# Choice of attention heads split over three steps, weight loads spread between block moves, and v evacuated by ScalarE and POOL, in a four-layer attention and MoE kernel

## The chip, the cores and the metric

The kernel runs on one core of one Trainium2 chip. The metric is device time in microseconds (us), lower is better. The core's engines are TensorE (PE, with its weight loads shown apart as PEld), VectorE (DVE), ScalarE (ACT), GpSimd (POOL) and SyncE (SP), which here only issues DMAs and loads registers.

## The reference, cut to what matters

The input is x of 2 batches x 1024 tokens x 256 features. Four layers, each with a layer norm ahead and a residual add behind, run one after the other: (a) cross attention of 16 heads to 77 context tokens, (b) a self attention that chooses 4 of 16 heads for each batch, (c) a GELU layer whose two weight matrices are the context, (d) a top-1 mixture of 8 experts. The change concerns (b):

```python
def _L0_ffn_ref(x, Wq, bq, Wk, bk, Wv, bv, Wr, br, Wo, bo):   # x: layer norm of the residual, (2, 1024, 256)
    dist = softmax(mean(x @ Wr + br, axis=1), axis=-1)          # one distribution over 16 heads for each batch
    _, idx = top_k(dist, 4)
    idx = sort(idx, axis=-1)
    Q, K, V = proj(Wq, bq), proj(Wk, bk), proj(Wv, bv)          # 16 heads of 64
    Qs, Ks, Vs = gather(Q), gather(K), gather(V)                # the 4 chosen heads of each batch
    score = softmax(einsum('bhqd,bhkd->bhqk', Qs, Ks) / 8, axis=-1)
    O = einsum('bhqk,bhkd->bhqd', score, Vs)
    return O.transpose(0, 2, 1, 3).reshape(b, s, 256) @ Wo + bo
```

A batch's heads can be chosen only when all its 1024 tokens have left layer (a); the kernel then loads the weights of the four chosen heads only.

## The kernel before

**Tiling.** Tokens are cut into 16 tiles of 128 (8 for each batch), which lie in SBUF as `xs`. Layer (a) is a pipeline of 20 calls `a_step(s)` (L507): each runs the scores of tile s, the transposes of tile s-1, the values of tile s-2, the output's transpose of tile s-3 and its projection `po_a` of tile s-4 (added into `xs` by VectorE, L505). Layer (b) is a pipeline of 36 calls `b_step(s)` (L821). Its unit i is one query tile of 128 with one pair of heads, 32 units in all: sixteen of the first batch, then sixteen of the second. Layers (c) and (d) are pieces spread over the b-steps; the expert blocks (L1199 to L1230) come after the last one. The program is one straight line of instructions on each engine.

**What b_step(s) does, in order.** PE: scores of unit s (`bsc`, L721, four matmuls of 512 columns into two PSUM buffers of tag `big`). VectorE: transposes in place, in 32x32 blocks, of the second head of unit s-1 (`be`, L748). In every second step: the move of two units' transposed weights from `be` to `beT` across partitions, 16 DMAs issued by SP (`b_moved`, L750 to L761), and reciprocals of the softmax sums, spread by POOL (`brb`, L781). Then the evacuations that stand in the list `due`, which the step before put there, on ACT. Then for each of the two heads VectorE's negated row maximum (`bnm`, L737) and ACT's exponential from PSUM into `be` (L739). Then PE's values of unit s-4 (`bov`, L769, 64 matmuls that read `beT` and `v`) and VectorE's normalization (`boT`, L797). Every second step PE turns the sums (`brt`) and multiplies a finished tile by the output weights (`po_b`). Last, VectorE transposes the first head of unit s. `be` and `beT` have two buffers each, so the move before last must have read `be` before exponentials can write it again; the PSUM tags `big`, `tr` and `acc` have two buffers each, and `bov`, `po_b` and `v` share `acc`.

**What sets the order.** It is written out by hand. `at(stage, s, pos, f, ...)` (L1281) puts a call in the plan, `take` (L1284) runs the calls of a position: position 0 comes after the `due` evacuations and ahead of the exponentials, 2 behind the values, 3 ahead of the step's last transposes. `piece(f, ...)` (L1321) runs the PE part of f at once and appends its evacuation to `due`, so that it runs at the next step's start. The Python order is the order of each engine's queue.

**The choice of heads.** `route_sums` (L542) and `route_mean` (L551) sum a batch's normalized rows; `route_logits` (L559) multiplies by the router and takes the exponential; `route_heads` (L572) does the rest on VectorE: `rp`, `lg`, `top`, `idx` (L574 to L580), the sort of four indices by rank (L582 to L599), then on SP, for each chosen head, a register load (L609) and one DMA of 64 KB for each of k, q and v (L614) and one for the bias of v (L625), 16 in all, and last on VectorE the chosen heads' biases by a one-hot sum (`hot`, `hb`, `hs_`, `bc`, L628 to L645). For the first batch this is planned in a-step 14, for the second in b-step 3. The weights' tiles `ws_k`, `ws_q`, `ws_v` and `bvs` have one buffer each.

**q, k and v.** `b_qk(b, k, m, n)` (L648) makes 512 tokens of q or k for head pair m in one PSUM bank by two matmuls, evacuated with bias by ACT. `b_v(b, t)` (L674) makes v of one tile for all four heads; with `later` ACT copies it out of PSUM (L692) and POOL adds the bias (L693), without it VectorE does both in one add (L688). The second batch's v goes the first way, the first batch's the second way. The first batch's scores begin with b-step 0, the second's with b-step 16; values follow four steps later.

Of the kernel before, what the change touches and what calls it, by code (L numbers as in the profile page):

```python
# [9 lines left out]
F32 = mybir.dt.float32  # L10
# [8 lines left out]
SP = (mybir.EngineType.SP,)  # L19

P = 128
# [18 lines left out]
def kernel(  # L40
# [30 lines left out]
    nc = tc.nc  # L71
# [3 lines left out]
    C = D // P  # L75
# [13 lines left out]
    NH = f_wr.shape[1]  # L89
    FD = f_wq.shape[1] // NH  # L90
    NA = f_wo.shape[0] // FD
# [24 lines left out]
    wsp = early.enter_context(tc.tile_pool(name="wsp", bufs=1))  # L116
# [94 lines left out]
    for c0, c1, off0 in ((0, NCH - 1, 0), (NCH - 1, NCH, off_c[-1])):  # L211
        hs = hsel[:, c0:c1, :]
# [359 lines left out]
    def route_heads(b):  # L572

        lg, sm = sel[b]  # L574
        rp = small.tile([P, 1], F32, name=f"rp_{b}", tag="rp")
        nc.vector.reciprocal(rp, sm)
        nc.vector.tensor_scalar(lg, lg, rp, None, ALU.mult)
        top = small.tile([P, 8], F32, name=f"top_{b}", tag="top")
        idx = small.tile([P, 8], U32, name=f"idx_{b}", tag="idx")
        nc.vector.max(top, lg)  # L580
        nc.vector.max_index(idx, top, lg)

        fi = small.tile([P, NA], F32, name=f"fi_{b}", tag="fi")
# [17 lines left out]
        w = {  # L601
            k: wsp.tile([P, C, NA, FD], F32, name=f"ws_{k}{b}", tag=f"ws_{k}") for k in "qkv"
        }
        bv = wsp.tile([P, NA, FD], F32, name=f"bvs_{b}", tag="bvs")
        hs = {}

        def load(s, *what):
            if s not in hs:
                hs[s] = nc.values_load(seli[0:1, s : s + 1], engines=SP, min_val=0, max_val=NH - 1)  # L609
            for k in what:  # L610
                v = {"k": f_wk, "q": f_wq, "v": f_wv}[k].rearrange(
                    "(c p) (h d) -> p c h d", p=P, h=NH
                )
                nc.sync.dma_start(w[k][:, :, s : s + 1, :], v[:, :, bass.ds(hs[s], 1), :])  # L614

        load(0, "k", "q")
        load(1, "k", "q")
        load(2, "k")
        load(3, "k", "q")
        load(2, "q")  # L620
        for s in range(NA):
            load(s, "v")
        v = f_bv.rearrange("(h d) -> h d", h=NH)
        for s in range(NA):
            nc.sync.dma_start(bv[:, s, :], v[bass.ds(hs[s], 1), :].to_broadcast([P, FD]))  # L625
# [12 lines left out]
        nc.vector.tensor_reduce(  # L638
            hs_.rearrange("p k m h -> p (k m h)"), hb.rearrange("p k s n -> p (k s) n"),
            AX.X, ALU.add,  # L640
        )
        bc = wsp.tile([P, 2, NP], F32, name=f"bc_{b}", tag="bc", bufs=2)
        for h in range(2):
            r = slice(h * FD, h * FD + FD)
            nc.vector.tensor_copy(bc[r], hs_[r, :, :, h])  # L645
        sel[b] = w, {"k": bc[:, 0, :], "q": bc[:, 1, :]}, bv

    def b_qk(b, k, m, n, pool=accp, ptag="acc", later=False):  # L648

# [631 lines left out]
    def at(stage, s, pos, f, *args):  # L1281
        plan.setdefault((stage, s, pos), []).append((f, args))
# [70 lines left out]
    stages = [("a", s) for s in range(T + 4)] + [("b", s) for s in range(1, NI)]  # L1353
    for b in range(B):
        for i in range(4):
            s = b * NT + 2 * i + 5
            t0 = b * NT + 2 * i
            at(*stages[s], 3, do_rows, "b", t0, fbo_b)
            at(*stages[s + 1], 3, do_turn, "b", t0)
            at(*stages[s + 2], 1 if stages[s + 2][0] == "a" else 3, route_sums, b, i)  # L1360
        s = b * NT + 13
        at(*stages[s], 1 if b == 0 else 3, route_mean, b)
    at("a", 13, 3, route_logits, 0)
    at("a", 14, 1, route_heads, 0)
    at("b", 3, 2, route_logits, 1)
    at("b", 3, 3, route_heads, 1)
    for s, args in (
        (15, (0, "k", 0, 0)), (16, (0, "k", 0, 512)), (16, (0, "q", 0, 0)), (17, (0, "k", 1, 0)),
        (17, (0, "k", 1, 512)), (18, (0, "q", 1, 0)),
# [1 line left out]
        at("a", s, 3, b_qk, *args)  # L1371
    tr = (trp, "tr")
    acc = (accp, "acc")
    at("b", 2, 3, b_qk, 0, "q", 0, 512)
    at("b", 3, 3, b_qk, 0, "q", 1, 512)
    for t in range(NT):
        at(*(("a", 18, 3), ("a", 18, 3), ("b", 0, 3), ("b", 0, 3),
             ("b", 1, 2), ("b", 1, 3), ("b", 2, 2), ("b", 2, 3))[t], b_v, 0, t, *(acc if t > 3 else tr))
    for s, k, m, n in (
        (5, "k", 0, 0), (6, "k", 0, 512), (6, "q", 0, 0), (7, "k", 1, 0), (8, "k", 1, 512),  # L1380
        (9, "q", 1, 0), (18, "q", 0, 512), (20, "q", 1, 512),
    ):
        at("b", s, 3, piece, b_qk, 1, k, m, n, *tr)
    for t in range(NT):
        at("b", (10, 12, 13, 14, 15, 16, 17, 18)[t], 3, piece, b_v, 1, t, *acc)

    gelus = {}

# [9 lines left out]
    for g in range(3):  # L1398
        s, t0 = 4 * g, TG * g
# [13 lines left out]
    for t0 in (6, 8):  # L1413
        s = 2 * t0
# [12 lines left out]
    t0 = T1 - 2  # L1427
# [16 lines left out]
    t0 = T1  # L1444
# [197 lines left out]
```

## Time and profile before

| | us |
|---|---|
| median of 3 runs (lowest, highest) | 607.15 (604.54, 609.48) |
| the profiled execution: its time, its span | 606.1, 604.4 |
| PE busy (share of the span) | 536.2 (89%) |
| PEld busy | 408.3 (68%) |
| VectorE busy | 378.8 (63%) |
| ScalarE busy | 206.7 (34%) |
| POOL busy | 176.2 (29%) |
| mean granted PE clock | 0.935 of full speed |
| exponentials (L739), 64, each | 1.114 |
| row maxima (L737), 64, each | 1.212 |
| block transposes (L748), 64, each | 1.221 |
| values `bov` (L769), 1024 matmuls, each | 0.291 |
| scores `bsc` (L721), 256 matmuls, each | 0.661 |

The profile is of one execution; the span runs from its first to its last instruction, and all times "at" some point are counted from the span's start. Busy times are sums of the instructions' durations. "A <- B" in the waits reads: idle time of A's group that ended when B finished; the numbers behind it are the total, the count and the longest, in us. "x16" behind a row is the number of instructions in it. A granted clock of 0.50 means that PE ran at half speed in that stretch.

### The profile page before, as it was taken

Reading aid. Unit: us, or ns where it says so; the run is one execution under the profiler, and the core shown is the slowest. Engines: PE = TensorE matmul, PEld = TensorE weight load, DVE = VectorE, ACT = ScalarE, POOL = GpSimd, SP = SyncE. Lnnn points to the kernel's source line nnn. Section 1 sums busy time; section 2 is a strip of 40 time slices with the busy share of each in tenths; the row PEclk is TensorE's granted clock in tenths of the full one; section 3 lists DMA queues with packets and bytes.
Section 4 is the critical chain, followed back from the end, with each engine's and each line's share of the span. In section 5 each row is a group of like instructions: output and inputs, shape, how many; then the busy total and the mean of one; then the engine's idle time right before and its main releaser. Section 6 shows DMA issues by size and latency. Waiting matters only on the chain. (4 is left out here: it accounts for less than half of the span.)

```text
span 604.4 us, 10406 instructions
## 1 busy us (share of the span) xinstructions
PE 536.2 (89%) x3706; PEld 408.3 (68%) x3706; DVE 378.8 (63%) x894; ACT 206.7 (34%) x440; POOL 176.2 (29%) x225
## 2 busy tenths in 40 slices
PE   5999999989896599999998995794896899999994
PEld 4577878876444355666755563584786799999994
DVE  6767667862788367888888898765356233333341
ACT  3555555543343244555554443210210011111110
POOL 6646233433200001344623412003110232333221
PEclk9999999999987799999999996857797899999998
DMA  8000000020062956787686884569954599999940
GB/s 252 22 2 1 1 1 2 1 56 7 2 139 59 207 127 154 166 183 187 142 199 154 199 208 104 136 145 334 375 197 165 193 338 325 355 376 352 351 145 15
DMA packets 61707, 96.34 MB, mean 159 GB/s; under 512 B 15352, under 2 KB 46547, under 8 KB 61653
## 3 DMA queue, kind: packets, MB, share of 16 engines
q1 hardware_dynamic: 58384, 87.61, 51.9%
q0 software_dynamic: 2560, 7.34, 3.3%
q8 instruction: 31, 0.51, 0.4%
q10 hardware_dynamic: 709, 0.68, 0.3%
q14 instruction: 23, 0.19, 0.1%
HBM read 55.76 MB, written 6.82 MB: 104 GB/s over the span
## 5 line engine op out<-in xcount | busy, mean ns | idle before, releaser
L739 ACT ACTIVATE be<-bsc,bnm 128x1024 f32<-128x1024 f32 x64 | 71.3, 1114 | 107.3 <-DVE bnm L737 88.8
L737 DVE TENSOR_REDUCE bnm<-bsc 128x1 f32<-128x1024 f32 x64 | 74.9, 1212 | 23.6 <-PE bsc L721 23.6
L769 PEld LDWEIGHTS bov<-beT,v 128*64 128x64 f32 x1024 | 61.0, 147 | 36.0 <-issue 22.9
L721 PE MATMUL bsc<-kT,qT 64*128 64x512 f32 x256 | 76.0, 661 | 6.3 <-ACT be L739 6.3
L769 PE MATMUL bov<-beT,v 128*64 128x128 f32 x1024 | 68.8, 291 | 11.5 <-DMA beT<-be 7.9
L1218 PE MATMUL epo<-w2s,ehT 128*128 128x256 f32 x320 | 77.9, 387 | 0.0
L1199 PE MATMUL ph<-ybT,w1s 128*128 128x128 f32 x640 | 76.9, 278 | 1.0 <-DVE ybT L1184 1.0
L1199 PEld LDWEIGHTS ph<-ybT,w1s 128*128 128x128 f32 x640 | 76.0, 194 | 2.4 <-DVE ybT L1184 1.4
L748 DVE STREAM_TRANSPOSE be<-be 128x1024 f32<-128x1024 f32 x64 | 75.8, 1221 | 1.6 <-DMA beT<-be 1.1
L1206 ACT ACTIVATE ehT<-ph,b1s 128x128 f32<-128x128 f32 x80 | 22.9, 369 | 120.3 <-PE ph L1199 120.3
L1218 PEld LDWEIGHTS epo<-w2s,ehT 128*128 128x128 f32 x320 | 59.2, 195 | 6.8
L721 PEld LDWEIGHTS bsc<-kT,qT 64*128 64x128 f32 x256 | 27.5, 198 | 37.9 <-issue 18.0
L1208 DVE TENSOR_SCALAR ehT<-ph,b1s 128x128 f32<-128x128 f32 x80 | 22.5, 343 | 48.8 <-ACT ehT L1206 48.6
L1230 POOL DMA_INDIRECT out_dram<-ob,etok x20 | 20.4, 1018 | 93.9 <-DMA out_dram<-ob,etok 37.3
L478 PE MATMUL av<-vblk,eT 128*128 128x51 f32 x320 | 37.4, 272 | 0.8 <-DVE hn L486 0.8
L478 PEld LDWEIGHTS av<-vblk,eT 128*128 128x128 f32 x320 | 37.1, 192 | 1.6 <-DVE hn L486 1.1
L454 DVE TENSOR_REDUCE mx<-sc 128x8 f32<-128x616 f32 x32 | 25.3, 792 | 16.6 <-PE sc L440 16.6
L781 POOL COPY brb<-brc 128x256 f32<-128x256 f32 x16 | 6.4, 400 | 97.1 <-DVE brc L779 97.1
L470 ACT COPY eT<-pt 128x512 f32<-128x512 f32 (+1 forms) x48 | 23.0, 515 | 25.9 <-PE pt L469 25.3
L456 DVE TENSOR_TENSOR e<-sc,mx 128x616 f32<-128x616 f32 x32 | 25.6, 799 | 1.7
L291 POOL TENSOR_TENSOR rs_b<-rs_b,minus_half 128x2 f32<-128x2 f32 x8 | 5.7, 713 | 71.7 <-DVE rs_b L290 53.7
L460 ACT ACTIVATE e<-e 128x616 f32<-128x616 f32 x32 | 23.0, 723 | 9.4 <-DVE e L456 9.3
(260 smaller groups left out, 818.2 us busy)
## 6 DMA issues: line engine op xcount, KB each, us to landing
beT<-be SPq DMA_DIRECT2D x256, 128.0 KB
w1s<-in_L_ffn_w_dram SPq DMA_DIRECT2D x20, 1024.0 KB
w2s<-in_L_ffn_w_dram SPq DMA_DIRECT2D x20, 1024.0 KB
b2s<-in_L_ffn_b_dram SPq DMA_DIRECT2D x20, 128.0 KB
xs<-in_x_dram SPq DMA_DIRECT2D x4, 512.0 KB
ztok<-y_d SPq DMA_DIRECT2D x8, 256.0 KB
ztok<-xs SPq DMA_DIRECT2D x8, 256.0 KB
ws_k<-in_L_ffn_Wk_dram SPq DMA_DIRECT2D x8, 64.0 KB
```

The source lines that it names most:

```text
L454: nc.vector.tensor_reduce(mx, scv, AX.X, ALU.max)
L456: nc.vector.tensor_tensor(em.rearrange("p (g h) k -> p g h k", g=2), scv, mx.unsqueeze(3).to_broadcast([P, 2, HG, KC]), ALU.subtract,)
L460: nc.scalar.activation(em, em, AF.Exp)
L470: copy(eTs[t][:, c0 : c0 + n, :], pt[:, :n, :])
L478: nc.tensor.matmul(av[:, h0 : h0 + HW, :].rearrange("p h d -> p (h d)"), lhsT=eT[:, c, :], rhs=vblk[:, t // NT, c].rearrange("p h d -> p ( ...
L721: nc.tensor.matmul(sc[h][:, n : n + 512], lhsT=qks[b, "q", m][r, q0 : q0 + P], rhs=qks[b, "k", m][r, n : n + 512], start=True, stop=True,)
L737: nc.vector.tensor_reduce(nm, sc[h], AX.X, ALU.max, negate=True)
L739: nc.scalar.activation(bes[gm][:, :, q, h, :], sc[h].rearrange("p (g x) -> p g x", g=QD), AF.Exp, bias=nm, accum_out=sms[g][:, q, s : s + 1],)
L748: nc.vector.transpose(e, e)
L769: nc.tensor.matmul(ov[h * FD : (h + 1) * FD, :].rearrange("p (g x) -> p g x", g=QD), lhsT=vs[g * TG // NT][:, k, 2 * m + h, :], rhs=eT[:, ...
L1199: nc.tensor.matmul(ph[:, f, :], lhsT=ws[n][0][:, c, f * P : (f + 1) * P], rhs=ybT[:, c, :], start=(c == 0), stop=(c == C - 1),)
L1218: nc.tensor.matmul(po, lhsT=hT[:, f, :], rhs=w2s[:, f, :], start=(f == 0), stop=(f == FC - 1))
```

## The change

There are four edits.

- `route_heads` becomes a generator in parts. For the first batch all its parts are still taken in a-step 14. For the second batch the logits move from position 2 of b-step 3 to position 0; the choice of the indices is taken at (4, 0), the sort at (4, 2), the biases `hot` to `bc` at (5, 2), then the loads of the four k heads with their register loads at (6, 0), of q at (8, 0), of v at (10, 0) and of the bias of v at (12, 0). A generator's step runs up to the next `yield`, so the part up to `idx` is the first `next`, and so on. Position 0 of an even step comes behind the move that the same step issues.
- For the first batch k and q are loaded head by head, then v; the biases `hot` to `bc` are computed ahead of the loads for both batches.
- The first batch's v tiles all become pieces: two in a-step 18, two each in b-steps 0, 1 and 2, evacuated by ACT and POOL. Its last two q groups move from b-steps 2 and 3 to pieces in 4 and 5. The transposes of second-batch rows (`do_turn "b"`) that fall in b-steps become pieces too.
- The second batch's k and q groups move from steps 5, 6, 6, 7, 8, 9, 18, 20 to 8, 9, 10, 12, 13, 14, 20, 22, its v tiles from 10, 12, 13, 14, 15, 16, 17, 18 to 13, 13, 14, 15, 16, 17, 17, 19.

```diff
@@ -579,6 +579,7 @@
         idx = small.tile([P, 8], U32, name=f"idx_{b}", tag="idx")
         nc.vector.max(top, lg)
         nc.vector.max_index(idx, top, lg)
+        yield
 
         fi = small.tile([P, NA], F32, name=f"fi_{b}", tag="fi")
         nc.vector.tensor_copy(fi, idx[:, :NA])
@@ -598,11 +599,34 @@
         seli = small.tile([P, NA], I32, name=f"seli_{b}", tag="seli")
         nc.vector.tensor_copy(seli, se)
 
+        yield
+
+        hot = wsp.tile([P, NA, NH], F32, name=f"hot_{b}", tag="hot", bufs=1)
+        nc.vector.tensor_tensor(
+            hot, iota16.unsqueeze(1).to_broadcast([P, NA, NH]),
+            se.unsqueeze(2).to_broadcast([P, NA, NH]), ALU.is_equal,
+        )
+        hb = wsp.tile([P, 2, NA, NH], F32, name=f"hb_{b}", tag="hb", bufs=1)
+        nc.vector.tensor_tensor(
+            hb, hot.unsqueeze(1).to_broadcast([P, 2, NA, NH]),
+            hbT.unsqueeze(2).to_broadcast([P, 2, NA, NH]), ALU.mult,
+        )
+        hs_ = wsp.tile([P, 2, NP, 2], F32, name=f"hs_{b}", tag="hs", bufs=1)
+        nc.vector.tensor_reduce(
+            hs_.rearrange("p k m h -> p (k m h)"), hb.rearrange("p k s n -> p (k s) n"),
+            AX.X, ALU.add,
+        )
+        bc = wsp.tile([P, 2, NP], F32, name=f"bc_{b}", tag="bc", bufs=2)
+        for h in range(2):
+            r = slice(h * FD, h * FD + FD)
+            nc.vector.tensor_copy(bc[r], hs_[r, :, :, h])
+        yield
         w = {
             k: wsp.tile([P, C, NA, FD], F32, name=f"ws_{k}{b}", tag=f"ws_{k}") for k in "qkv"
         }
         bv = wsp.tile([P, NA, FD], F32, name=f"bvs_{b}", tag="bvs")
         hs = {}
+        sel[b] = w, {"k": bc[:, 0, :], "q": bc[:, 1, :]}, bv
 
         def load(s, *what):
             if s not in hs:
@@ -613,37 +637,15 @@
                 )
                 nc.sync.dma_start(w[k][:, :, s : s + 1, :], v[:, :, bass.ds(hs[s], 1), :])
 
-        load(0, "k", "q")
-        load(1, "k", "q")
-        load(2, "k")
-        load(3, "k", "q")
-        load(2, "q")
-        for s in range(NA):
-            load(s, "v")
+
+        for ks in (("k", "q"), ("v",)) if b == 0 else ("k", "q", "v"):
+            for s in range(NA):
+                load(s, *ks)
+            if b:
+                yield
         v = f_bv.rearrange("(h d) -> h d", h=NH)
         for s in range(NA):
             nc.sync.dma_start(bv[:, s, :], v[bass.ds(hs[s], 1), :].to_broadcast([P, FD]))
-
-        hot = wsp.tile([P, NA, NH], F32, name=f"hot_{b}", tag="hot", bufs=1)
-        nc.vector.tensor_tensor(
-            hot, iota16.unsqueeze(1).to_broadcast([P, NA, NH]),
-            se.unsqueeze(2).to_broadcast([P, NA, NH]), ALU.is_equal,
-        )
-        hb = wsp.tile([P, 2, NA, NH], F32, name=f"hb_{b}", tag="hb", bufs=1)
-        nc.vector.tensor_tensor(
-            hb, hot.unsqueeze(1).to_broadcast([P, 2, NA, NH]),
-            hbT.unsqueeze(2).to_broadcast([P, 2, NA, NH]), ALU.mult,
-        )
-        hs_ = wsp.tile([P, 2, NP, 2], F32, name=f"hs_{b}", tag="hs", bufs=1)
-        nc.vector.tensor_reduce(
-            hs_.rearrange("p k m h -> p (k m h)"), hb.rearrange("p k s n -> p (k s) n"),
-            AX.X, ALU.add,
-        )
-        bc = wsp.tile([P, 2, NP], F32, name=f"bc_{b}", tag="bc", bufs=2)
-        for h in range(2):
-            r = slice(h * FD, h * FD + FD)
-            nc.vector.tensor_copy(bc[r], hs_[r, :, :, h])
-        sel[b] = w, {"k": bc[:, 0, :], "q": bc[:, 1, :]}, bv
 
     def b_qk(b, k, m, n, pool=accp, ptag="acc", later=False):
 
@@ -1356,14 +1358,26 @@
             s = b * NT + 2 * i + 5
             t0 = b * NT + 2 * i
             at(*stages[s], 3, do_rows, "b", t0, fbo_b)
-            at(*stages[s + 1], 3, do_turn, "b", t0)
+            if stages[s + 1][0] == "a":
+                at(*stages[s + 1], 3, do_turn, "b", t0)
+            else:
+                at(*stages[s + 1], 3, piece, do_turn, "b", t0)
             at(*stages[s + 2], 1 if stages[s + 2][0] == "a" else 3, route_sums, b, i)
         s = b * NT + 13
         at(*stages[s], 1 if b == 0 else 3, route_mean, b)
     at("a", 13, 3, route_logits, 0)
-    at("a", 14, 1, route_heads, 0)
-    at("b", 3, 2, route_logits, 1)
-    at("b", 3, 3, route_heads, 1)
+    heads = {}
+
+    def route_part(b):
+        if b not in heads:
+            heads[b] = route_heads(b)
+        next(heads[b], None)
+
+    for _ in range(4):
+        at("a", 14, 1, route_part, 0)
+    at("b", 3, 0, route_logits, 1)
+    for s, pos in ((4, 0), (4, 2), (5, 2), (6, 0), (8, 0), (10, 0), (12, 0)):
+        at("b", s, pos, route_part, 1)
     for s, args in (
         (15, (0, "k", 0, 0)), (16, (0, "k", 0, 512)), (16, (0, "q", 0, 0)), (17, (0, "k", 1, 0)),
         (17, (0, "k", 1, 512)), (18, (0, "q", 1, 0)),
@@ -1371,18 +1385,18 @@
         at("a", s, 3, b_qk, *args)
     tr = (trp, "tr")
     acc = (accp, "acc")
-    at("b", 2, 3, b_qk, 0, "q", 0, 512)
-    at("b", 3, 3, b_qk, 0, "q", 1, 512)
+    for s, m in ((4, 0), (5, 1)):
+        at("b", s, 3, piece, b_qk, 0, "q", m, 512, *tr)
     for t in range(NT):
-        at(*(("a", 18, 3), ("a", 18, 3), ("b", 0, 3), ("b", 0, 3),
-             ("b", 1, 2), ("b", 1, 3), ("b", 2, 2), ("b", 2, 3))[t], b_v, 0, t, *(acc if t > 3 else tr))
+        s = ("a", 18) if t < 2 else ("b", t // 2 - 1)
+        at(*s, 3, piece, b_v, 0, t, *(tr if t < 2 else acc))
     for s, k, m, n in (
-        (5, "k", 0, 0), (6, "k", 0, 512), (6, "q", 0, 0), (7, "k", 1, 0), (8, "k", 1, 512),
-        (9, "q", 1, 0), (18, "q", 0, 512), (20, "q", 1, 512),
+        (8, "k", 0, 0), (9, "k", 0, 512), (10, "q", 0, 0), (12, "k", 1, 0), (13, "k", 1, 512),
+        (14, "q", 1, 0), (20, "q", 0, 512), (22, "q", 1, 512),
     ):
         at("b", s, 3, piece, b_qk, 1, k, m, n, *tr)
     for t in range(NT):
-        at("b", (10, 12, 13, 14, 15, 16, 17, 18)[t], 3, piece, b_v, 1, t, *acc)
+        at("b", (13, 13, 14, 15, 16, 17, 17, 19)[t], 3, piece, b_v, 1, t, *acc)
 
     gelus = {}
```

More of the change, by code (lines that the diff above doesn't have):

```diff
@@ L599, in route_heads @@
         nc.vector.tensor_copy(seli, se)
[L601 to L612, printed above, removed]
-                )
-                nc.sync.dma_start(w[k][:, :, s : s + 1, :], v[:, :, bass.ds(hs[s], 1), :])
-        load(0, "k", "q")
-        load(1, "k", "q")
-        load(2, "k")
-        load(3, "k", "q")
-        load(2, "q")
-        for s in range(NA):
-            load(s, "v")
-        v = f_bv.rearrange("(h d) -> h d", h=NH)
-        for s in range(NA):
-            nc.sync.dma_start(bv[:, s, :], v[bass.ds(hs[s], 1), :].to_broadcast([P, FD]))
+        yield
         hot = wsp.tile([P, NA, NH], F32, name=f"hot_{b}", tag="hot", bufs=1)
@@ L645, in route_heads, with load @@
             nc.vector.tensor_copy(bc[r], hs_[r, :, :, h])
-        sel[b] = w, {"k": bc[:, 0, :], "q": bc[:, 1, :]}, bv
+        yield
+        w = {
+            k: wsp.tile([P, C, NA, FD], F32, name=f"ws_{k}{b}", tag=f"ws_{k}") for k in "qkv"
+        }
+        bv = wsp.tile([P, NA, FD], F32, name=f"bvs_{b}", tag="bvs")
+        hs = {}
+        sel[b] = w, {"k": bc[:, 0, :], "q": bc[:, 1, :]}, bv
+        def load(s, *what):
+            if s not in hs:
+                hs[s] = nc.values_load(seli[0:1, s : s + 1], engines=SP, min_val=0, max_val=NH - 1)
+            for k in what:
+                v = {"k": f_wk, "q": f_wq, "v": f_wv}[k].rearrange(
+                    "(c p) (h d) -> p c h d", p=P, h=NH
+                )
+                nc.sync.dma_start(w[k][:, :, s : s + 1, :], v[:, :, bass.ds(hs[s], 1), :])
+        for ks in (("k", "q"), ("v",)) if b == 0 else ("k", "q", "v"):
[3 more added lines that the diff above has]
+                yield
+        v = f_bv.rearrange("(h d) -> h d", h=NH)
+        for s in range(NA):
+            nc.sync.dma_start(bv[:, s, :], v[bass.ds(hs[s], 1), :].to_broadcast([P, FD]))
     def b_qk(b, k, m, n, pool=accp, ptag="acc", later=False):
```

## The prediction

> **What bounds the kernel now.** I read the share of each engine by slices first, then a sum by stretches, then the waits, then SP's and VectorE's rows around the one hole. I call step s the call `b_step(s)` and date it by its first `bnm` (L737): steps 0 to 12 start at 154.42, 161.91, 170.35, 176.89, 186.64, 192.94, 200.04, 216.81, 223.58, 230.17, 236.07, 242.43, 247.25 us, step 13 at 254.66, step 18 at 285.73, step 24 at 328.04. Step 6 lasts 16.8 us, where the others last 5 to 8.
>
> ```profile
> 152.40:216.80 64.40, 48.80 (x223) 25.06 (x224) 42.32 (x70) 20.79 (x38) 5.61 (x7) 0.84 0.50 112
> 216.80:297.60 80.80, 79.95 (x643) 52.27 (x643) 68.21 (x97) 43.17 (x87) 27.17 (x34) 1.00 0.74 164
> ```
>
> The columns are the length, then the busy time of PE, PEld, DVE, ACT and POOL, then PE's clock, DMA share and rate. After 216.8 PE is busy 79.95 of 80.80 us: there PE's work sets the time. Before it PE idles 15.6 us and runs partly at half clock. So what an edit saves before 216.8 counts only less the PE work that it pushes behind that point.
>
> ```profile
> DVE boT L797 <- PE bov L769: 11.1, 4, 8.9
> PE bov L769 <- DMA beT<-be: 7.9, 2, 7.5
> PE bsc L721 <- ACT be L739: 6.3, 3, 4.7
> ```
>
> The hole is PE waiting 7.5 us for a move (`beT<-be`), with VectorE waiting 8.9 us behind it. The 4.7 us are one step before: scores 5 wait for the exponentials of step 4. Why both, the timelines of SP and VectorE show (start, time from the first to the last of the group, instruction):
>
> ```profile
> 169.51 10.12 SPq L758 DMA_DIRECT2D beT<-be  x16
> 183.98 0.39 SPq L614 DMA_DIRECT2D ws_k<-in_L_ffn_Wk_dram  x1
> ...
> 193.58 1.91 SPq L625 DMA_DIRECT2D bvs<-in_L_ffn_bv_dram  x4
> 195.59 10.06 SPq L758 DMA_DIRECT2D beT<-be  x16
> ```
>
> The timeline of VectorE over the same stretch:
>
> ```profile
> 176.89 2.31 DVE L737 TENSOR_REDUCE bnm<-bsc 128x1 f32<-128x1024 f32 x2
> 179.13 0.15 DVE L565 TENSOR_TENSOR lg<-rps,br_b 128x16 f32<-128x16 f32 x1
> ...
> 184.29 2.37 DVE L748 STREAM_TRANSPOSE be<-be 128x1024 f32<-128x1024 f32 x2
> ```
>
> VectorE chooses the heads from 179.13 to 184.29 (5.16 us), and the transposes of step 3 wait behind it. Move 1 is ready at 186.6, but SP issues 16 weight and bias loads until 195.5, so it goes out at 195.59 and has landed by 207.5. A move costs SP 10.1 us (16 issues, one each 0.63 us).
>
> [...] the trace has clock 0.50 in 163.5 to 170.2, 187.4 to 194.1 and 204.5 to 211.1, each after PE idling. [...] v leaves PSUM by ScalarE and POOL adds the bias after; second batch's v does so here (374 ns L692, 732 ns L693).
>
> **The change, part by part.**
>
> First batch's v. Eight adds of 419 ns leave VectorE (about 0.34 us each in the queue, 2.7 us) for eight ACT copies of 374 ns and eight POOL adds of 732 ns, hidden on engines that are 34% and 29% busy. But the copies stand behind the step's exponentials on ACT. Copies 2 and 3 use the `acc` buffers, so `po_a` of the last attention tile now waits for copy 2: exponentials of step 0 end at 158.03, copy 158.4, `po_a` (1.03) 159.45, and VectorE's add (L505, at 159.08 before) 159.5. The two v adds saved in step 0 are eaten: step 1 at 162.35 (+0.45). In step 1 PE does both v tiles after `lps_b`, whose rows POOL delivers at 164.6; two tiles of 1.85 us at half clock, then scores 2: step 2 at 171.4 (+1.05). Were PE at full clock there, 169.3; I take 171.4 and keep 2 us for the range. Step 2 loses one 0.34 add twice but gets the two small logits operations and waits for them: 6.4 us, step 3 at 177.8.
>
> Choice of heads in three parts. Step 3 keeps 0.94 us of the 5.16 (reciprocal to index, 180.76 to 181.70), after its transposes. Exponentials of step 3 end at 181.45, transposes at 182.65: move 1 is ready at 182.65, 3.9 us sooner, and SP is empty (move 0 done about 177.4). Step 4 starts at 183.65. Step 4: bnm 2.27, boT 0.22, second part 1.4 (181.72 to 183.04 and its gap), transposes 2.3: 6.2. Step 5: 2.27, 0.22, third part 1.25, 2.3, reciprocal: 6.1. Steps 5 and 6 start at 189.85 and 195.95. The two q matmul groups that come to steps 4 and 5 (1.81 each) fit, PE having 3.8 of 6.2 us to do. Move 1 lands at 182.7 + 10.1 + 1.8 = 194.6 (1.8 from last issue to use, 205.65 to 207.5), before it is needed: the 7.5 and 4.7 us are gone. Step 6 has then only 4.9 us of VectorE work: step 7 at 200.85 against 216.81, 16.0 us sooner.
>
> Loads behind the moves. Each kind must go out before the next move. From before: a k head with its register load 1.16 us (186.77 to 187.93), four 4.65; q, v 0.555 each, four 2.2; bias 0.525, four 2.1. Move 2 is ready at 195.95 and issues to 206.15, landing 207.95. k goes to 210.8; move 3 is ready by 205.8 but goes 210.9 to 221.3, landing 223.1; q to 223.5, move 4 to 233.9, landing 235.7; v to 236.1 (one slow issue of 1.3 could add 1), move 5 to about 247, landing 248.7. Who waits: `bov` of steps 8, 10 and 12, and the exponentials of those steps, whose `be` buffer the move two before must have left. PE at step 8 is through its scores at 206.1 and waits 1.85 us; then po_b 0.87, k 1.81 (landing taken as in time; batch 0's were used 3.4 us after issue, a bound of 1.3 us late), scores 1.92: step 9 at 214.2. Step 10 at 220.1, `bov` waits for 223.1; step 11 at 229.0; step 12 at 234.1 (13.2 sooner), `bov` waits 1.4 for 235.7; step 13 at 243.0 (11.7 sooner). Move 5 meets no waiter.
>
> Work moved later. From step 13 on PE carries what before was done: k and q of head pair 1 (two groups of 1.81) and two v tiles of 0.96, so 5.5 us. Summing PE by rows (bsc 1.92 + bov 1.90, po_b 0.87, brt 0.27, v 0.96, gps 0.96, gpo 0.87, lps 0.53), steps 13 to 17 take 7.8, 7.5, 6.4, 6.6, 6.5 = 34.8 us against 31.1 before, with PE always the longer chain: step 18 at 277.8, 7.9 sooner. Steps 18 to 23: the q groups move from 18 and 20 to 20 and 22; `bov` of step 20 waits about 1.2 us for the last v, whose POOL add stands behind `rs_d`, `y_d`, brb and xs (0.71, 2.43, 0.40, 0.73). Each step's longer chain of PE and VectorE sums to 42.1 against 42.3: step 24 at 319.9, 8.1 sooner. Behind it the program is the same; I take 8.0. Span 604.4 - 8.0 = 596.4, that run 606.1 - 8.0 = 598.1. The median, 607.15, lies 1.05 above that run: 599.2.
>
> **Rivals.** Case 1, above: 5.5 to 10.5 us gained, 596.7 to 601.7. For it speaks that every wait removed is on VectorE's, SP's or PE's own rows.
>
> Case 2, more is kept: steps 1 and 2 at full clock (2 us), and the waits of steps 8 to 12 hidden. Then the 16.0 less three groups of 1.81 pushed past step 7, 10.6, and 2: 12.6 us, 594.5. For it: PE has about 1 us of slack in 80. Against: SP's back-to-back moves.
>
> Case 3, the wait returns on SP: moves 3, 4 and 5 take 11.5 us in place of about 10.3 (before, moves took 10.0 to 11.8 in this stage), 3.6 us later landing; 4.4 kept, 602.8. For it: the DMA share is 0.9 and more while a move runs. Against: moves 1 and 2 ran back to back at 10.06.
>
> Case 4, not faster: PE's clock. Waits of 1.85, 3 and 1.4 us in steps 8, 10 and 12 each halve it[...] (6.7 us in the rows before), each costing 3.4 us of PE work, 10.2 in all; against 8.0 kept, 2.2 slower, 609.4. It decides only if all three trip and none of the loss hides in the wait for the next move. Against: the waits are shorter than the ones of before that tripped (7.5 and 4.7), though one of about 2 us did.
>
> That the order doesn't come about is excluded by the instruction order of the changed kernel: loads stand after moves 2, 3, 4 and 5.
>
> **The numbers.** Chances 0.58, 0.14, 0.20, 0.08. One per cent, 6.1 us, is about what a measurement can tell from no change. Of case 1 nine tenths lie beyond it: faster 0.52 + 0.14 = 0.66; same 0.06 + 0.20 + 0.03 = 0.29; slower 0.05. The range reaches from case 2's value, 594.5, into case 3, 605.5, and leaves out case 4 and the ends of 2 and 3, under 2 in 10.
>
> **What would show it.** Right: SP's row has sixteen moves from about 182.7 with no load ahead; no `bov` wait over 3 us in steps 4 to 7; step 7 near 201; k between moves 2 and 3 in 4.65 us; step 13 near 243 and step 18 near 278. Wrong: step 4 after 186; waits for `beT` in steps 8 to 12 that sum to over 8 us, or clock 0.50 there; the gain of step 13 kept whole at step 24 (PE then had slack), or lost there.

## The result, and the profile after

The changed kernel takes 602.63 us (median of 18 runs, 598.72 to 607.89) against 605.78 us for the kernel before (18 runs, 601.60 to 609.48). The ratio is 0.9946, 95% interval 0.9921 to 0.9971: faster by 3.15 us, where the forecast had 8.0. The ratio leaves out one slow execution of the changed kernel, the one of 607.89 us. The profiled execution took 604.26 us, its span is 602.6.

The first view is the sum by stretches, cut at the steps' own starts (steps 0, 7, 13, 18 and 24), since two kernels can't be compared over equal times. First the kernel before, columns as in the prediction:

```profile
154.42:216.81 62.39, 46.79 (x214) 24.28 (x216) 41.90 (x70) 20.79 (x38) 5.61 (x7) 0.84 0.52 116
216.81:254.66 37.85, 37.85 (x292) 23.08 (x294) 30.97 (x40) 19.96 (x39) 8.60 (x12) 1.00 0.64 141
254.66:285.73 31.07, 30.22 (x250) 20.41 (x250) 27.70 (x42) 16.91 (x35) 12.62 (x16) 1.00 0.80 179
285.73:328.04 42.31, 39.98 (x337) 27.29 (x338) 36.39 (x66) 21.31 (x43) 18.87 (x22) 1.00 0.74 169
```

The changed kernel, the same stages:

```profile
155.17:202.61 47.44, 38.26 (x199) 21.17 (x200) 39.95 (x64) 20.82 (x41) 9.77 (x13) 0.89 0.48 105
202.61:246.64 44.03, 37.98 (x290) 22.13 (x290) 31.39 (x40) 20.16 (x38) 7.15 (x10) 1.00 0.78 171
246.64:281.99 35.35, 34.65 (x268) 22.88 (x270) 27.90 (x42) 19.12 (x39) 14.15 (x18) 1.00 0.72 165
281.99:325.07 43.08, 41.04 (x348) 27.51 (x349) 36.48 (x65) 21.21 (x43) 18.70 (x22) 1.00 0.70 159
```

Steps 0 to 6 are 15.0 us shorter. Steps 7 to 12 give back 6.2, and PE's busy time in them is the same (37.98 against 37.85), so all of it is waiting: 6.05 us idle where there was none. Steps 13 to 17 give back 4.3, and there PE is busy 4.4 us longer: this is the work pushed behind. Steps 18 to 23 cost 0.8. At step 24 3.0 us are left.

What PE waits for in steps 7 to 12 of the changed kernel (us, times, longest; the kernel before has no such row in its steps 7 to 12):

```profile
PE bov L771 <- DMA beT<-be: 4.4, 2, 2.2
PE bov L771 <- DVE bnm L739: 1.3, 1, 1.3
PE bps_k L658 <- DMA ws_k<-in_L_ffn_Wk_dram: 0.4, 1, 0.4
```

The second row is most likely a move as well: the values read `beT` and not the row maximum that the row names (it ends at 209.72), and they start at 209.79, 1.84 us after the end of move 2's last issue (207.95), where those of step 12 start 1.96 us after the end of move 4's. SP's timeline of the changed kernel shows why moves are late now (start, first to last of the group):

```profile
168.10 39.85 SPq L760 DMA_DIRECT2D beT<-be  x48
208.98 3.88 SPq L638 DMA_DIRECT2D ws_k<-in_L_ffn_Wk_dram  x4
212.97 10.05 SPq L760 DMA_DIRECT2D beT<-be  x16
223.21 2.12 SPq L638 DMA_DIRECT2D ws_q<-in_L_ffn_Wq_dram  x4
225.44 11.68 SPq L760 DMA_DIRECT2D beT<-be  x16
237.65 2.05 SPq L638 DMA_DIRECT2D ws_v<-in_L_ffn_Wv_dram  x4
239.81 11.38 SPq L760 DMA_DIRECT2D beT<-be  x16
251.44 1.94 SPq L648 DMA_DIRECT2D bvs<-in_L_ffn_bv_dram  x4
```

The order is the one forecast: k behind move 2, q behind move 3, and so on. But each row starts where the one above ends: from 197.9 (move 2) to 263.6 (end of move 6) SP never stands still. SP's own waits say it in one row. Changed kernel, 195 to 265 us:

```profile
SPq L760 <- DVE be L750: 10.2, 2, 5.2
```

Kernel before, 195 to 275 us:

```profile
SPq L758 <- DVE be L748: 13.3, 5, 5.9
```

Before, SP stood waiting for VectorE's transposes five times, 13.3 us in all, 10.9 of them ahead of moves 3 to 6: that was slack of the queue on which the loads now lie (12.4 us). After, there are two waits, 5.0 us before move 2 and 5.2 us after move 6, and none between. The best number for the gain is therefore not step 7's start (14.2 us sooner) but move 2's (205.8 before, 197.9 after: 7.9 us), because behind move 2 SP's sum alone sets when moves 3 to 6 go out; at move 6 it is 6.4 (259.9, 253.5). At step 24, behind the work pushed there, 3.0 are left.

### The profile page after: what moved, and what is told of

Read it like the earlier page. It is cut to its first block, busy times and chain, and to the rows that moved or that the text cites. A ratio compares the mean times of both kernels' runs of the same rounds, so it can differ in the third digit from the quotient of the medians.

```text
span 602.6 us, 10413 instructions
## 1 busy us (share of the span) xinstructions
PE 532.2 (88%) x3706; PEld 404.5 (67%) x3706; DVE 376.8 (63%) x886; ACT 209.6 (35%) x448; POOL 181.7 (30%) x233
## 5 line engine op out<-in xcount | busy, mean ns | idle before, releaser
L771 PEld LDWEIGHTS bov<-beT,v 128*64 128x64 f32 x1024 | 57.5, 141 | 33.6 <-issue 20.8
L723 PE MATMUL bsc<-kT,qT 64*128 64x512 f32 x256 | 73.8, 656 | 4.3 <-ACT be L741 4.3
L771 PE MATMUL bov<-beT,v 128*64 128x128 f32 x1024 | 65.4, 281 | 9.1 <-DMA beT<-be 4.9
L1210 DVE TENSOR_SCALAR ehT<-ph,b1s 128x128 f32<-128x128 f32 x80 | 22.5, 344 | 41.5 <-ACT ehT L1208 41.4
L1172 POOL DMA_INDIRECT zb<-ztok,etok x20 | 19.6, 981 | 22.7 <-PE epo L1220 15.6
```

Of the source, the lines that this page charges most:

```text
L723: nc.tensor.matmul(sc[h][:, n : n + 512], lhsT=qks[b, "q", m][r, q0 : q0 + P], rhs=qks[b, "k", m][r, n : n + 512], start=True, stop=True,)
L771: nc.tensor.matmul(ov[h * FD : (h + 1) * FD, :].rearrange("p (g x) -> p g x", g=QD), lhsT=vs[g * TG // NT][:, k, 2 * m + h, :], rhs=eT[:, ...
```

## The experiments

All start from the changed kernel unless said otherwise. Ratios are to the kernel before on the same chip, from 5 to 22 runs of each kernel. The steps are read from one trace of each (us from the span's start). In the expectations, theory A says that SP's queue, with the loads on it, makes the moves late and PE wait for them; rival B says that something else does.

| kernel | move 2 starts | step 7 | step 13 | step 18 | step 24 | ratio (95% interval) |
|---|---|---|---|---|---|---|
| before | 205.8 | 216.81 | 254.66 | 285.73 | 328.04 | 1 |
| changed | 197.9 | 202.61 | 246.64 | 281.99 | 325.07 | 0.9946 (0.9921 to 0.9971) |
| changed, again | 197.7 | 202.45 | 246.57 | 281.92 | 325.00 | 0.9929 (0.9901 to 0.9957) |
| no loads | 197.3 | 202.02 | 241.68 | 277.03 | 320.12 | not comparable |
| loads on ScalarE | 197.4 | 202.08 | 251.92 | 287.27 | 330.35 | 1.0026 (1.0006 to 1.0046) |
| groups in the waits | 197.4 | 202.10 | 245.30 | 279.17 | 322.27 | 0.9908 (0.9876 to 0.9941) |
| loads in one lump | 195.6 | 200.33 | 250.94 | 286.29 | 329.39 | 1.0041 (1.0022 to 1.0061) |
| k loads in SP's gap | 198.0 | 202.62 | 242.70 | 278.05 | 321.14 | 0.9884 (0.9851 to 0.9917) |
| and groups sooner | 199.2 | 203.40 | 242.99 | 276.99 | 319.12 | 0.9827 (0.9805 to 0.9849) |
| and v loads later | 199.0 | 203.44 | 242.85 | 276.04 | 318.16 | 0.9820 (0.9788 to 0.9853) |
| choice unsplit | 197.1 | 203.24 | 245.15 | 280.50 | 323.59 | 0.9895 (0.9873 to 0.9918) |
| choice unsplit, again | 198.0 | 204.54 | 246.20 | 281.55 | 324.64 | 0.9956 (0.9933 to 0.9979) |
| v by VectorE | 195.9 | 200.57 | 245.91 | 281.26 | 324.34 | 0.9931 (0.9908 to 0.9954) |
| loads' part alone | 198.3 | 203.93 | 246.68 | 282.03 | 325.11 | 0.9968 (0.9949 to 0.9986) |

Behind step 24 these programs are the same (but for "no loads"). That rest took from 274.8 to 279.7 us in the profiled executions, 277.5 and 276.7 in the two of the changed kernel, so a stage table settles more than one span does.

**Is it SP's queue?** The loads are taken out: the second batch uses the first batch's weights, so its values differ.

```diff
+        if b:
+            sel[b] = sel[0][0], {"k": bc[:, 0, :], "q": bc[:, 1, :]}, sel[0][2]
+            return
```

> The second batch's sixteen weight and bias loads and their four register loads are left out; its q, k and v are made with the first batch's weights, which alters its values. Everything else stands where the changed kernel has it. Theory A (the loads on SP's queue keep the block moves late: SP works without a gap from 197.9 to 263.6 us there, and steps 7 to 12 wait 6.05 us on PE): moves 3 to 6 start when their step is ready, PE's idle time in steps 7 to 12 falls from 6.1 to under 2 us, step 13 starts near 241 in place of 246.6 and the whole is 4 to 6 us shorter than the changed kernel's 602.6, 597 to 598. Rival B (the loss after step 7 is the k, q and v work pushed behind it, or a chain of VectorE and ScalarE that makes the moves ready late, so SP only looks busy): step 13 within 1.5 us of 246.6 and the time within 1.5 us of 602.6.

Step 13 starts at 241.68, as theory A had it. PE's waits in steps 7 to 12 of this kernel:

```profile
PE bov L775 <- DVE bnm L743: 1.3, 1, 1.3
PE bov L775 <- DMA beT<-be: 0.4, 1, 0.4
```

Moves 3 to 5 start at 207.5, 220.8 and 233.1, each within 0.2 us of its last transpose, and PE is idle 1.7 us in place of 6.05. The forecast of the whole time failed for a reason of its own: other values route the tokens to other experts, and the one branch of the program, which stands in the last layer, then adds three expert blocks, so that there are 736 first-layer matmuls in place of 640 (639.01 us, median). So only the steps count, 5.0 us up to step 24. B is refuted for steps 7 to 12.

**The same loads from another queue.** Register loads and DMAs go to ScalarE, two heads at a time behind the exponentials.

```diff
-        nc.sync.dma_start(w[k][:, :, s : s + 1, :], v[:, :, bass.ds(hs[s], 1), :])
+        (nc.scalar if b else nc.sync).dma_start(w[k][:, :, s : s + 1, :], v[:, :, bass.ds(hs[s], 1), :])
...
-    for s, pos in ((4, 0), (4, 2), (5, 2), (6, 0), (8, 0), (10, 0), (12, 0)):
+    for s, pos in ((4, 0), (4, 2), (5, 2), (6, 2), (7, 2), (8, 2), (8, 2), (10, 2), (10, 2), (11, 2)):
```

> The second batch's loads, with their register loads, are issued from ScalarE's queue behind the exponentials of steps 6 to 11 in place of SP's queue behind the moves; k, q and v groups stay where the changed kernel has them. Theory A (SP's queue is what is short in steps 7 to 13): as with no loads at all, PE idle in steps 7 to 12 under 2.5 us, step 13 near 241 to 242, time 597.5 to 599. Rival B (not SP): no gain, and ScalarE, which gets about 0.55 us for a load and 1.16 with a register load, delays evacuations: 602 to 604. A third way, A right but ScalarE's exponentials late by the 2.3 us that two k heads take: 600 to 601.

608.14 us: a miss of all three. SP's waits from 195 to 245 us name something none of them had:

```profile
SPq L761 <- DMA ws_v<-in_L_ffn_Wv_dram: 3.3, 3, 1.7
SPq L761 <- DMA ws_k<-in_L_ffn_Wk_dram: 2.0, 2, 1.5
SPq L761 <- DMA bvs<-in_L_ffn_bv_dram: 2.0, 2, 1.7
SPq L761 <- DMA ws_q<-in_L_ffn_Wq_dram: 1.1, 2, 0.8
```

SP's moves wait 8.4 us for loads that ScalarE issues, though a move reads and writes none of the tiles that these loads fill; what ties the two together, the rows don't show. Of the 12.4 us taken off SP, 8.4 came back as waits. PE waits 3.9 us for move 2 and 4.1 us for move 4, and step 13 starts 5.3 us later than in the changed kernel. The run doesn't speak against A, since it replaced one wait on SP's queue by another; it doesn't test A either.

**Loads in one lump.** All sixteen behind move 2.

```diff
         for ks in (("k", "q"), ("v",)) if b == 0 else ("k", "q", "v"):
             for s in range(NA):
                 load(s, *ks)
-            if b:
-                yield
```

> The changed kernel with all sixteen loads together behind move 2 in step 6, in place of one kind behind each of moves 2, 3, 4 and 5. Theory A: SP has 12.3 us of loads ahead of move 3, which starts near 220 in place of 213.0 and lands near 232, so that the values of step 10 wait some 9 us; but moves 4 to 6 have no loads ahead, and SP's sum to the end of move 6 is the same: step 14 starts 1 to 3 us after 255.2, time 603.5 to 605.5. Rival C (kind by kind is what makes the gain): the one long wait is kept whole, step 14 5 us or more after 255.2, time 607 or more. Rival B: time within 1.5 us of 602.6.

609.43 us; step 14 starts at 259.53, 4.3 us later than in the changed kernel. That lies between A's 1 to 3 us and rival C's 5 or more; the time is C's. A's sum is wrong: the long wait is not made good. PE's row at move 3, and then the stretch from 224 to 235 us:

```profile
229.49 3.68 PE L769 MATMUL bov<-beT,v 128*64 128x128 f32 x32 [8.57 <-DMA beT<-be]
```

```profile
224.00:235.00 11.00, 5.51 (x35) 4.30 (x36) 1.47 (x6) 2.30 (x4) 0.06 (x1) 0.53 0.86 187
```

After 8.57 us of waiting the values take 3.68 us in place of 1.97, the clock being 0.50 from 224.5 for 10.2 us. Step 11 then starts at 237.8, so move 5's transposes are ready only at 242.7 while SP is free from 239.4: the late steps put a gap of 3.4 us into the queue that A took as full. The changed kernel's waits of 1.3 to 2.2 us between steps 7 and 18 come with no half clock (1.00), but this isn't safe: in two of the runs below waits as short came with one, and the clock is 0.50 from 237.7 and from 226.6 for 3.41 us. The values behind them, in the run with v by VectorE and in the second one with the choice unsplit:

```profile
236.72 2.75 PE L771 MATMUL bov<-beT,v 128*64 128x128 f32 x32 [1.89 <-DMA beT<-be]
225.20 2.43 PE L771 MATMUL bov<-beT,v 128*64 128x128 f32 x32 [1.98 <-DMA beT<-be]
```

Kind by kind is worth 4.3 us up to step 14, by the clock and by SP's gap; how much is due to each is not told apart.

**PE's waits filled.** Four groups go ahead of the values of steps 10 to 13.

```diff
-        (8, "k", 0, 0), (9, "k", 0, 512), (10, "q", 0, 0), (12, "k", 1, 0), (13, "k", 1, 512),
-        (14, "q", 1, 0), (20, "q", 0, 512), (22, "q", 1, 512),
+        (8, "k", 0, 0), (9, "k", 0, 512), (20, "q", 0, 512), (22, "q", 1, 512),
...
+    for s, k, m, n in ((10, "k", 1, 0), (11, "k", 1, 512), (12, "q", 0, 0), (13, "q", 1, 0)):
+        at("b", s, 0, piece, b_qk, 1, k, m, n, *tr)
```

> The changed kernel with four of the second batch's groups (k of head pair 1, then q of both pairs) moved from the ends of steps 10, 12, 13, 14 to places ahead of the values of steps 10, 11, 12, 13, where PE waits for a move. Theory A: the moves stay where they are, PE fills its two waits of 2.2 us in steps 10 and 12 with this work, and steps 13 and 14 are lighter by it: step 14 starts 3 to 4 us before 255.2 and the time is 599 to 600. Rival B (the waits are a consequence of a slow chain through PE itself): whatever is put ahead of the values makes them later by as much, step 14 near 255 and the time 602 to 604.

600.94 us. Step 14 starts at 253.77, 1.5 us sooner and not 3 to 4; 2.8 us are left at step 24. Half of the expected gain goes to waits that the edit makes itself: more pieces want the two `tr` buffers, and PE waits 1.1 us at `lps_c` in step 11 and 0.5 at `brt` in step 13, both for ScalarE's evacuations.

**k loads in SP's gap.** SP stands idle for 5.0 us between moves 1 and 2, and the k loads take 5.0.

```diff
-    for s, pos in ((4, 0), (4, 2), (5, 2), (6, 0), (8, 0), (10, 0), (12, 0)):
+    for s, pos in ((4, 0), (4, 2), (5, 2), (5, 2), (8, 0), (10, 0), (12, 0)):
```

> The changed kernel with one thing moved: the four k loads and their register loads (5.0 us of SP) go out at the end of step 5, between moves 1 and 2, where SP stands idle from 192.9 to 197.9 us, and not behind move 2. q, v, bias and all groups on PE stay. Theory A (SP's queue is what is short from move 2 to move 6): move 2 starts near 197.9 as before, move 3 near 208 in place of 213.0, the value wait of step 10 (2.2 us) goes and that of step 12 falls to about 1, step 13 starts near 243 in place of 246.6; time 3 to 4 us under the changed kernel, 598.5 to 599.5. Rival B (the loads' place on SP is not what holds steps 9 to 13): step 13 within 1 us of 246.6, time 602 to 603.5. Third way: k loads from 192.9 make move 2 late; then step 8's values wait and the gain is lost.

599.43 us, and step 13 at 242.70: A's numbers. SP's timeline of this kernel:

```profile
182.72 10.14 SPq L760 DMA_DIRECT2D beT<-be  x16
193.95 3.94 SPq L638 DMA_DIRECT2D ws_k<-in_L_ffn_Wk_dram  x4
198.00 21.61 SPq L760 DMA_DIRECT2D beT<-be  x32
219.80 2.10 SPq L638 DMA_DIRECT2D ws_q<-in_L_ffn_Wq_dram  x4
```

The k loads end at 197.9, the moment at which move 2 is ready, so they cost nothing there, and moves 2 and 3 follow one another. One line moved gives 3.9 us at step 24, more than the whole change kept.

**And the groups sooner.** As that kernel, with k groups in steps 6 to 9, q of pair 1 ahead of the values of step 12, and the last v tile in step 18 in place of 19.

```diff
+        (6, "k", 0, 0), (7, "k", 0, 512), (9, "k", 1, 512),
+        (10, "q", 0, 0), (20, "q", 0, 512), (22, "q", 1, 512),
...
+    for s, k, m, n in ((8, "k", 1, 0), (12, "q", 1, 0)):
+        at("b", s, 0, piece, b_qk, 1, k, m, n, *tr)
...
-        at("b", (13, 13, 14, 15, 16, 17, 17, 19)[t], 3, piece, b_v, 1, t, *acc)
+        at("b", (13, 13, 14, 15, 16, 17, 17, 18)[t], 3, piece, b_v, 1, t, *acc)
```

> As the run with the k loads between moves 1 and 2, and the second batch's k groups also made sooner (steps 6, 7, 8, 9 in place of 8, 9, 12, 13, q of pair 1 ahead of the values of step 12), the last v tile in step 18 in place of 19. Theory A: PE's holes of steps 6 to 12 (6 us) are filled and what the change had pushed behind step 13 comes back ahead of it; step 18 starts 5 to 6 us before 282.0, time 596 to 598. Rival B (PE work put into steps 6 to 9 only lengthens them, since PE and VectorE are both full there): no better than the run with the loads alone.

596.04 us; step 18 at 276.99, 5.0 us before the changed kernel. PE's work in steps 13 to 17 is down from 34.65 to 31.18 us, so what was pushed behind has come back; but PE idles 2.8 us there, and the steps take 34.0 us in place of 35.35. Steps 18 to 23 take 42.13 us in place of 43.09 in the run before, where the v tile that moved is one of the changes.

**And the v loads later.** In that kernel the v and bias loads and the v tiles come later.

```diff
-    for s, pos in ((4, 0), (4, 2), (5, 2), (5, 2), (8, 0), (10, 0), (12, 0)):
+    for s, pos in ((4, 0), (4, 2), (5, 2), (5, 2), (8, 0), (12, 0), (14, 0)):
...
-        at("b", (13, 13, 14, 15, 16, 17, 17, 18)[t], 3, piece, b_v, 1, t, *acc)
+        at("b", (14, 14, 15, 16, 16, 17, 17, 18)[t], 3, piece, b_v, 1, t, *acc)
```

> The kernel with the k loads between moves 1 and 2 and the earlier groups, and besides the four v loads behind move 5 in place of move 4, the bias loads behind move 6 in place of move 5, v tiles from step 14 in place of 13. Theory A: move 5 starts at once when it is ready, near 234.6 in place of 237.3, the 1.7 us that the values of step 14 wait in that kernel go, step 18 starts 1 to 2 us before 277.0, time 594 to 595.5. Rival: PE is full there and the wait had been filled by other work later; 595.5 to 597.

594.56 us, 11 us under the kernel before on that chip (605.53). By the ratio it can't be told from the kernel ahead of it (0.9820 and 0.9827); by the steps, step 18 comes 0.95 us sooner, the lower end of what was expected. Move 5 starts at 234.5. Its stretches from step 7 to 13 and 13 to 18:

```profile
203.44:242.85 39.41, 39.41 (x293) 22.74 (x294) 31.08 (x40) 20.57 (x39) 7.18 (x10) 1.00 0.86 188
242.85:276.04 33.19, 32.29 (x260) 21.70 (x262) 28.02 (x41) 17.91 (x37) 14.10 (x18) 1.00 0.75 174
```

PE is busy all of steps 7 to 12 again, as it was before the change.

**The other parts.** The choice whole in step 3 (run twice), the first batch's v by VectorE, the loads' part alone, and the changed kernel once more as a ruler.

```diff
-    at("b", 3, 0, route_logits, 1)
-    for s, pos in ((4, 0), (4, 2), (5, 2), (6, 0), (8, 0), (10, 0), (12, 0)):
+    at("b", 3, 2, route_logits, 1)
+    for s, pos in ((3, 3), (3, 3), (3, 3), (6, 0), (8, 0), (10, 0), (12, 0)):
```

> The changed kernel with the choice of heads whole in step 3 as before (logits behind the values, then all 18 small VectorE operations and the biases ahead of step 3's transposes), loads, groups and v as changed. If the split is worth what the forecast took (5.2 us of VectorE in one place make move 1 3.9 us late, less the 2.6 us that the parts cost in steps 4 and 5): step 4 starts near 188 and step 7 1.3 to 3 us after 202.6, time 604 to 606. If only the loads' place behind the moves matters: step 7 within 0.7 us of 202.6, time 602 to 603.

> The changed kernel with the choice of heads whole in step 3, for a second time, beside the changed kernel on one chip. Theory (SP has no gap from move 2 to move 6, so only move 2's start counts for what follows, and the split does not make move 2 ready sooner: 197.0 unsplit, 197.9 split): equal to the changed kernel within 1.5 us. Rival: the split costs 2 us (its parts stand in three steps ahead of transposes): unsplit shorter by 1.5 to 2.5 us. Other rival: the split gains its 3 us of steps 3 to 6: unsplit longer by 2 us or more.

600.76 and 603.92 us. The two differ more from each other (0.9895 and 0.9956) than from the changed kernel (0.9946, 0.9929), so no effect on the time can be told. Beside the changed kernel on one chip the unsplit one is 2.45 us longer (603.92, 601.47), as the rival of a gain by the split had it, but the intervals overlap, and the first run, which lies under both its expectations, points the other way. The steps tell more. From step 2 to step 7 the unsplit kernels take 34.3 and 33.4 us, the changed one 31.4 and 31.3: the split does save some 2.5 us there. Then steps 7 to 12 take 41.9 and 41.7 us against 44.0 and 44.1, and the saving is gone: move 2 starts at 197.1 and 198.0 unsplit, 197.9 and 197.7 split. What comes behind it, up to step 24, is SP's.

```diff
-        s = ("a", 18) if t < 2 else ("b", t // 2 - 1)
-        at(*s, 3, piece, b_v, 0, t, *(tr if t < 2 else acc))
+        at(*(("a", 18, 3), ("a", 18, 3), ("b", 0, 3), ("b", 0, 3),
+             ("b", 1, 2), ("b", 1, 3), ("b", 2, 2), ("b", 2, 3))[t], b_v, 0, t, *(acc if t > 3 else tr))
```

> The changed kernel with the first batch's eight v tiles taken out of PSUM by VectorE again, at the places of the kernel before; all else as changed. By the forecast the 2.7 us of adds that leave VectorE in steps 0 to 2 are eaten by waits behind ScalarE's copies: steps 0 to 3 last 22.5 us either way (22.47 before, 22.54 changed), step 7 and the time within 1 us of 202.6 and 602.6. Rival: the edit does save VectorE's 2.7 us (step 3 then later by 2 to 3 us, time 605). Other rival: the copies on ScalarE cost (step 0 starts 0.75 us sooner, and the time is 601).

602.65 us. Steps 0 to 2 take 21.8 us; with the copies on ScalarE they took 22.5 in the changed kernel, and 20.9 to 23.6 in others with the same code there. Within that spread no worth of the edit can be told, and the ratio (0.9931) lies between the two of the changed kernel (0.9929, 0.9946), as forecast. The half clock named above falls into its step 12, which takes 11.5 us (10.2 in the changed kernel).

```diff
-    for s, m in ((4, 0), (5, 1)):
-        at("b", s, 3, piece, b_qk, 0, "q", m, 512, *tr)
+    for s, m in ((2, 0), (3, 1)):
+        at("b", s, 3, b_qk, 0, "q", m, 512)
```

(with both edits above, and the second-batch turns at once rather than as pieces)

> The kernel before with one part of the change alone: the second batch's loads one kind at a time behind moves 2, 3, 4 and 5, with its k, q and v groups at the changed kernel's later places (they cannot run ahead of their weights). The choice of heads stays whole in step 3, the first batch's v goes through VectorE, its last two q groups stay in steps 2 and 3. Theory: this part is the whole gain: 600.5 to 603, as the changed kernel. Rival: split and v carry half of it: 604 to 605.5.

> The changed kernel once more, unaltered, as the ruler for the three runs beside it on this chip, and to see how far one execution's stages differ from another's: 601 to 604; every theory expects move 2 near 197 to 198, move 6 near 252 to 254, step 13 near 245 to 247.

603.98 us for the loads' part alone, 601.47 for the changed kernel beside it; their intervals (0.9949 to 0.9986, 0.9901 to 0.9957) overlap a little. By the time this lies between the two expectations, nearer to the rival's 604. Up to step 24 the two traces are equal: 325.11 and 325.00. So up to there the loads' place is the whole gain, and whether split and v add the other 2.5 us behind it, or the spread does, stays open. The ruler's stages agree with those of the first trace within 0.2 us.

## Why the prediction was right or wrong, by its own steps

**What bounds the kernel: right.** The 7.5 and 4.7 us waits are gone, and step 7 starts 14.2 us sooner. What the forecast's rows show of move 1 is SP's order of issuing (195.59, behind the last load at 195.49).

**First batch's v: right, the date partly by luck.** Step 2 was forecast at 171.4 and started at 171.20, and the run with VectorE shows no gain. But step 0 started 0.75 us later than before, and step 1 took 8.10 us and not 9.05; the half clock lasted 3.41 us there, 6.83 in the kernel before.

**Choice in three parts: mechanism right, worth wrong.** Move 1 went out at 182.66 (forecast 182.65). But parts two and three stand ahead of the transposes that move 2 waits for, and unsplit kernels have move 2 as early. The saving at step 7 was counted although SP takes it back before step 13.

**Step 4: mis-sized.** Forecast 6.2 us, measured 7.68. The row of its scores in the changed kernel:

```profile
180.28 4.91 PE L723 MATMUL bsc<-kT,qT 64*128 64x512 f32 x8 [2.64 <-ACT be L741]
```

The scores of one step, eight rows, take 4.91 us where they take 1.99 later; the clock is 0.50 from 179.2 to 186.0, which alone would make 3.98, and a second wait for ScalarE, whose next exponential ends at 181.3, lies among them. The values behind them then end at 187.5, and VectorE waits 1.18 us for them. I had put a half clock into steps 1 and 2 and none into step 4. Steps 0 to 6 came out 47.44 against 46.43.

**Loads behind the moves: the step that failed most.** It followed SP's queue correctly and mis-sized its terms, all but one in one direction (move 3 took 10.05 us, not 10.4). Move 2 starts at 197.9, not 196.05; k takes 5.0 us from move to move, not 4.65; q 2.4, not 2.2; move 4 11.68, not 10.4; v 2.7, not 2.2; move 5 11.38, not 10.9. Move 5 ends at 251.2, not 247, and since no gap is left in the queue nothing absorbs it: steps 7 to 12 took 44.03 against 42.15. Taking the loads out gives 5.0 us at step 13 and at step 24. What moves 4 and 5 take beyond 10.05 us is one slow issue each, 2.22 and 1.92 us in place of 0.59, each beside a packet of the queue `q8 instruction` (last section).

**Work moved later: nearly right.** Steps 13 to 17 took 35.35 against 34.8 forecast; 0.7 of it is `b_qk` of step 13 waiting for a `tr` buffer that VectorE's `g` still reads. Steps 18 to 23 took 43.08 against 42.1. `bov` of step 20 waits 1.15 us for the last v, as forecast, but the step is 1.8 us longer for it: 8.83 us with that tile in step 19, 7.02 with it in step 18 (the run with the groups sooner; step 18 is then 0.8 longer).

At step 24 the forecast had 8.1 us and 3.0 came: 5.1 are missing. These terms make 4.4 of them (1.0 + 1.9 + 0.55 + 1.0), and step 0, which started 0.75 us later than before, the rest; over the traces it started between 154.36 and 155.51.

**The rivals.** Case 3, the wait that returns on SP, gave 602.8 and had 0.20; the time came out at 602.63. That they agree so closely is luck: case 3 took 4.4 us off 607.15, the median of three runs, and the change took 3.15 off 605.78. Its mechanism holds for moves 4 and 5 (11.68 and 11.38 against its 11.5), while move 3 took 10.05; the longer loads and the later move 2 did the rest. The argument used against it (moves 1 and 2 ran at 10.06 back to back) was too few cases: the rows of the kernel before hold moves of 10.0 to 11.8 in just this stage. Case 4 did not come: the waits of 1.3 to 2.2 us came with no half clock, in part by luck, since waits of 1.89 and 1.98 us came with one in two runs. Case 2 needed waits hidden that were not. None of the prediction's signs of being wrong came: step 4 started at 184.09, the waits for moves in steps 8 to 12 sum to 5.7 us at clock 1.00, and the gain at step 13 (8.0 us) was neither kept whole nor lost at step 24. What failed were its signs of being right: k took 5.0 us and not 4.65, step 13 started at 246.64 and not near 243, step 18 at 281.99 and not near 278.

## What to carry to other kernels

A queue's slack is part of the forecast. Sum what an issuing engine has to do over the stage; where the sum fills it, the gain counts at the first transfer behind which it has no gap, not at the compute step that looks earlier. Then look for the queue's remaining gaps before moving work "behind" something: the same k loads took 5.0 us of SP in both places, but between moves 1 and 2 they delayed no move, and step 24 came 3.9 us sooner. And several short waits were better here than one long one (4.3 us), though a half clock came with waits of 1.89 and 1.98 us too.

## What the runs showed of the hardware that was not expected

- Single issues of a move take 1.0 to 2.3 us in place of 0.59 (the sixth of move 4 with 2.22, the fourteenth of move 5 with 1.92 us in the changed kernel). That is the whole difference between moves of 10.05 and of 11.4 to 11.7 us. Each lies beside a packet of the queue that the page of the changed kernel lists so (kind, packets, MB, share of the DMA engines):

```profile
q8 instruction: 31, 0.51, 0.4%
```

In the traces of the two kernels 17 issues of a move take 1.0 us or more, nine before and eight after the change. At each, one packet of this queue (16 KB) starts within 0.4 us of the issue's start, and the issue ends 0.15 to 0.38 us after the packet: in the changed kernel move 4's issue lasts from 228.53 to 230.75 and the packet from 228.66 to 230.39, move 5's from 248.00 to 249.93 and the packet from 248.13 to 249.56. In the kernel before, four such packets start between 221 and 270 us, and three of them lie beside issues of 1.36, 2.34 and 1.76 us, so the forecast could have counted them. Whether the packet makes the issue long, no run here shows.

- With the loads on ScalarE, SP's moves waited 8.4 us for the landing of loads that ScalarE had issued and whose tiles they neither read nor write.
- PE's half-clock stretches that end before the span does last 3.41, 6.83, 10.24 or 13.65 us in the traces of both kernels. In steps 0 to 6 they begin at 163.44, 187.33 and 204.40 us in the kernel before, and last 6.83 us each; in the changed kernel they begin at 165.55 and 179.21 us, and last 3.41 and 6.83. With the same code, steps 0 and 1 took from 14.4 to 17.1 us over the traces, a spread that no sum of durations holds.
